# A residual quantiser whose scores, residual and codeword sum are built in PSUM

## Chip, cores, metric

One core of a Trainium2 chip. The metric is device time of one launch in microseconds (us), the median of several runs. "Faster" or "slower" needs 2%.

Codes in the profile's views: PE is TensorE (PEld its weight loads), DVE VectorE, ACT ScalarE, POOL GpSimd and SP SyncE; "L696" is line 696 of the kernel. PSUM is the memory into which the kernel's matmuls write (pool `pp`), SBUF the one that holds its other tiles. "Granted clock" is the share of full clock that TensorE was given.

## The reference, cut to what matters

The program chains four residual blocks on a tensor of 4 images x 128 channels x 64 x 64 tokens. Only the last one is touched by the change: residual vector quantisation of the normalised tokens through 8 codebooks of 1024 words of 128 channels.

```python
for i in range(8):
    cb = codebooks[i]                                  # 1024 x 128
    d = sum(res * res, -1, keepdims=True) - 2.0 * einsum('ne,ke->nk', res, cb) \
        + sum(cb * cb, -1)[None, :]
    idx = argmin(d, axis=-1)
    dec = cb[idx]
    res = res - dec
    quant = quant + dec
# output: x + quant
```

Each stage needs the residual that the stage before left, so the 8 stages of a token are a chain. Different tokens are independent.

## The kernel before

The last layer takes tokens in groups of 512, two groups at a time, and each group in four tiles of 128 tokens. There are 4 x 8 groups x 8 stages x 4 = 1024 tiles. The stage, with cuts marked:

```python
def stage(self, i):
    sq = wp.tile([P, CH], F32, name="sq", bufs=2)
    nc.scalar.activation(sq, self.res, AF.Square)
    # ... n2 = -r.r of each token by four 128x1 matmuls, copied to nr2 ...
    pd = pp.tile([P, CH], F32, name="pd", bufs=1)
    for t in range(nt):
        ts = slice(t * P, (t + 1) * P)
        pe = pp.tile([P, NCODE], F32, name="pe", bufs=3)
        for h in range(NCODE // CH):
            hs = slice(h * CH, (h + 1) * CH)
            nc.tensor.matmul(pe[:, hs], self.res[:, ts], cbT[:, i, hs], start=True, stop=True)
        # minus the distance: 2 r.c - r.r - c.c
        d = wp.tile([P, NCODE], F32, name="d")
        nc.scalar.activation(d, pe, AF.Identity, bias=nr2[:, t : t + 1], scale=2.0)
        eng = nc.gpsimd if t % 2 else nc.vector
        eng.tensor_tensor(d, d, cb2[:, i, :], ALU.subtract)
        mx = wp.tile([P, 8], F32, name="mx")
        nc.vector.max(mx, d)
        idx = wp.tile([P, 8], U32, name="idx")
        nc.vector.max_index(idx, mx, d)
        dec = wp.tile([P, P], F32, name="dec")
        nc.gpsimd.indirect_dma_start(out=dec, ...)      # gathers 128 codewords
        nc.tensor.transpose(pd[:, ts], dec, cst.ident)
    # quant = pd, later quant += pd on VectorE (0.68 us)
    if i < NCB - 1:
        nc.vector.tensor_tensor(self.res, self.res, pd, ALU.subtract)
```

The order in which an engine runs its instructions is not that of this text. A scheduler decides it when the program is built, by priority and by its own guess of what is ready when. Each engine then works through its list.

## Time and profile before

| | before |
|---|---|
| time, us (median of 4 runs) | 18549.4 |
| the quantiser's part, from its first score matmul to the end | about 4240 |
| per tile | 4.14 |
| VectorE busy there | 81% |
| TensorE busy there, mean granted clock | 73%, 0.74 |

The groups, the window sums and a stretch of timeline are shown in the prediction. The view of waits from 15000 us to the end, 3.55 of the quantiser's 4.24 ms (who waited for whom: total us, times, longest us):

```profile
ACT d L701 <- PE pe L696: 843.2, 610, 4.9
...
ACT sq L682 <- DVE res L722: 703.0, 186, 7.9
...
POOL dec L711 <- DVE idx L709: 602.6, 256, 3.4
PE pd L716 <- DMA dec<-in_codebooks,idx: 556.7, 265, 4.6
...
PE pe L696 <- DVE res L722: 368.9, 186, 3.1
```

No single wait stands out. Every engine waits for the next link of the round trip at some time, and none is full.

### The profile page before, as it was taken

What the parts mean: (1) busy time and instruction counts of PE and PEld (TensorE: products, weight loads), DVE (VectorE), ACT (ScalarE), POOL (GpSimd) and SP (SyncE); (2) the same over time, 40 slices, a digit from 0 to 9 for tenths busy, and PEclk for the clock granted to TensorE, in tenths of its full rate; (3) what the DMA queues carried; (4) which work ended last, traced back from release to release, by engine and by line L of the source; (5) the groups of instructions that cost most, each with busy time, mean ns of one, the idle gap of its engine ahead of it and who ended that gap; (6) DMA issues with size and microseconds to landing.
All of it is one profiled execution on the core that took longest, in us unless ns stands there. A gap on an engine that the chain in (4) does not pass through costs nothing. (4 is left out here: it accounts for less than half of the span.)

```text
span 18551.7 us, 160743 instructions
## 1 busy us (share of the span) xinstructions
PE 14014.2 (76%) x63834; PEld 4562.7 (25%) x63834; DVE 15474.9 (83%) x11162; ACT 12396.8 (67%) x8354; POOL 4830.7 (26%) x2586
## 2 busy tenths in 40 slices
PE   6767776677778778787787877877777777777777
PEld 2222322223111111111111111111112333333333
DVE  7978788787888888888888888888888888888888
ACT  2323232333999999999999999999998323333332
POOL 4646465461000000000000000000001555555555
PEclk8888888888999999999999999999999777777777
DMA  0000000000000000000000000000000000000000
GB/s 19 0 0 0 0 0 0 0 0 2 1 1 1 1 1 1 1 1 1 1 1 1 1 1 1 1 1 1 1 1 12 19 17 18 18 18 18 18 19 18
DMA packets 42034, 99.52 MB, mean 5 GB/s; under 512 B 18368, under 2 KB 19136, under 8 KB 40768
## 3 DMA queue, kind: packets, MB, share of 16 engines
q0 software_dynamic: 32768, 67.17, 1.4%
q1 hardware_dynamic: 6208, 19.49, 0.3%
q8 instruction: 501, 8.21, 0.2%
q10 hardware_dynamic: 2304, 2.58, 0.0%
q14 instruction: 253, 2.07, 0.0%
HBM read 80.78 MB, written 8.39 MB: 5 GB/s over the span
## 5 line engine op out<-in xcount | busy, mean ns | idle before, releaser
L622 ACT ACTIVATE a<-pad,nw 128x2048 f32<-128x2048 f32 x5120 | 9706.1, 2000 | 18.7 <-PE acc L589 15.0
L589 PE MATMUL acc<-a,sel 128*32 128x512 f32 x40960 | 7012.0, 596 | 1974.7 <-ACT a L622 1974.7
L613 DVE SCALAR_TENSOR_TENSOR m<-pad,w,m 128x2048 f32<-128x2048 f32 x3072 | 6996.1, 2347 | 0.2
L589 PEld LDWEIGHTS acc<-a,sel 128*32 128x32 f32 x40960 | 1517.1, 109 | 7266.8 <-ACT a L622 4924.3
L696 PE MATMUL pe<-cbT,res 128*128 128x512 f32 x4096 | 2634.1, 780 | 496.4 <-DVE res L722 427.8
L664 POOL MEMSET minus<- 128x1 f32 x1 | 0.1, 99 | 9752.0 <-DVE xs L630 9752.0
L701 ACT ACTIVATE d<-pe,nr 128x1024 f32<-128x1024 f32 x1024 | 1131.6, 1114 | 2102.5 <-PE pe L696 968.2
L611 DVE TENSOR_SCALAR m<-pad,w 128x2048 f32<-128x2048 f32 x1024 | 1271.2, 1283 | 1498.6 <-PE acc L589 1498.6
L310 POOL TENSOR_TENSOR y<-y,hc 128x1024 f32<-128x1024 f32 x512 | 1435.8, 2804 | 1130.7 <-DVE hc L309 1123.2
L299 PE MATMUL pc<-xs,w_c 128*128 128x512 f32 x2048 | 1186.3, 709 | 694.6 <-DVE hc L309 694.6
L307 ACT COPY state<-h 128x1 f32<-128x1 f32 x512 | 97.7, 191 | 2112.6 <-DVE h L306 2112.6
L711 POOL DMA_INDIRECT dec<-in_codebooks,idx x1024 | 1146.0, 1119 | 1115.9 <-DVE idx L709 698.7
L707 DVE MAX8 mx<-d 128x8 f32<-128x1024 f32 x1024 | 1221.2, 1216 | 205.6 <-POOL d L705 201.2
L705 POOL TENSOR_TENSOR d<-d,cb 128x1024 f32<-128x1024 f32 x512 | 1210.8, 2366 | 621.1 <-ACT d L701 604.0
L696 PEld LDWEIGHTS pe<-cbT,res 128*128 128x128 f32 x4096 | 918.4, 251 | 1471.7 <-issue 1303.9
L306 DVE TENSOR_TENSOR_SCAN h<-da,state,db 128x1024 f32<-128x1024 f32 x384 | 1242.8, 3236 | 23.2 <-ACT da L301 0.5
L299 PE MATMUL pb<-xs,w_b 128*128 128x512 f32 x2048 | 1092.4, 657 | 194.9 <-DVE db L303 194.7
L709 DVE FIND_INDEX8 idx<-mx,d 128x8 uint32<-128x1024 f32 x1024 | 1238.9, 1219 | 0.0
L589 PE MATMUL acc<-m,sel 128*32 128x512 f32 x8192 | 1138.8, 592 | 1.2 <-DVE m L613 1.2
L705 DVE TENSOR_TENSOR d<-d,cb 128x1024 f32<-128x1024 f32 x512 | 740.7, 1455 | 144.8 <-ACT d L701 144.8
L716 PE MATMUL pd<-ident,dec 128*128 128x128 f32 x1024 | 346.9, 339 | 653.6 <-DMA dec<-in_codebooks,idx 639.8
L299 PEld LDWEIGHTS pc<-xs,w_c 128*128 128x128 f32 x2048 | 405.1, 214 | 1405.6 <-DVE hc L309 1025.9
(200 smaller groups left out, 9148.2 us busy)
## 6 DMA issues: line engine op xcount, KB each, us to landing
dec<-in_codebooks,idx POOLq DMA_INDIRECT x1024, 2.6
xs<-in_x SPq DMA_DIRECT2D x4, 2048.0 KB, 15.6
out<-quant SPq DMA_DIRECT2D x32, 256.0 KB, 2.0
cbT<-in_codebooksT ACTq DMA_DIRECT2D x4, 512.0 KB, 10.1
cbT<-in_codebooksT SPq DMA_DIRECT2D x4, 512.0 KB, 10.3
w<-in_adder SPq DMA_DIRECT2D x1, 576.0 KB, 3.6
fc2T<-in_fc2T ACTq DMA_DIRECT2D x1, 64.0 KB
projT<-in_projT ACTq DMA_DIRECT2D x1, 64.0 KB, 7.7
```

Of the source, the lines that this page charges most:

```text
L299: nc.tensor.matmul(ps[:, c], w[:, n, :], xs[:, c], start=True, stop=True)
L306: nc.vector.tensor_tensor_scan(h, da, db, first, ALU.mult, ALU.add)
L310: nc.gpsimd.tensor_tensor(y, y, hc, ALU.add)
L589: nc.tensor.matmul(acc[quad * j : quad * (j + 1), bk, :], sel[:, quad - 1 - i : 2 * quad - 1 - i], parts[j][:, bk * CH : (bk + 1) * CH], s ...
L611: nc.vector.tensor_scalar(m3, win(k, r0, rh), wk, None, ALU.max)
L613: nc.vector.scalar_tensor_tensor(m3, win(k, r0, rh), wk, m3, ALU.max, ALU.add)
L622: nc.scalar.activation(a.rearrange("p (h w) -> p h w", w=SIDE), win(k, r0, rh), AF.Abs, bias=nw[:, f, k : k + 1],)
L696: nc.tensor.matmul(pe[:, hs], self.res[:, ts], cbT[:, i, hs], start=True, stop=True)
L705: eng.tensor_tensor(d, d, cb2[:, i, :], ALU.subtract)
L707: nc.vector.max(mx, d)
L709: nc.vector.max_index(idx, mx, d)
L711: nc.gpsimd.indirect_dma_start(out=dec, out_offset=None, in_=table, in_offset=bass.IndirectOffsetOnAxis(ap=idx[:, 0:1], axis=0), element_o ...
```

## The change

The intent: ScalarE's pass over the scores and the subtraction on VectorE or GpSimd vanish. TensorE puts -c.c/2 into PSUM as a first matmul and adds r.c to it; VectorE's max and index search read PSUM. The residual and the sum of codewords are accumulated in PSUM too, by multiplying each gathered tile with minus identity and with identity. Score tiles have two PSUM buffers in place of three, since the residual and the sum now take room there too. Comments that the change strips are left out, as is the setup of `half` and `row`.

```diff
         def __init__(self, b, c):
             ...
-            self.quant = wp.tile([P, CH], F32, name="quant")
+            self.left = pp.tile([P, CH], F32, name="left")
+            nc.tensor.matmul(self.left, cst.ident, self.res, start=True, stop=False, ...)
+            self.quant = pp.tile([P, CH], F32, name="quant")
+            nc.tensor.matmul(self.quant, zero, self.res, start=True, stop=False, ...)

         def stage(self, i):
-            (square, n2 matmuls, nr2)
-            pd = pp.tile([P, CH], F32, name="pd", bufs=1)
+            last = i == NCB - 1
             for t in range(nt):
-                pe = pp.tile([P, NCODE], F32, name="pe", bufs=3)
+                pe = pp.tile([P, NCODE], F32, name="pe")          # bufs=2
+                for h in range(NCODE // CH):
+                    nc.tensor.matmul(pe[:, hs], row[:, i, :], half[:, hs], start=True, stop=False)
                 for h in range(NCODE // CH):
-                    nc.tensor.matmul(pe[:, hs], self.res[:, ts], cbT[:, i, hs], start=True, stop=True)
-                d = ...; nc.scalar.activation(d, pe, ...); eng.tensor_tensor(d, d, cb2[:, i, :], ALU.subtract)
+                    nc.tensor.matmul(pe[:, hs], self.res[:, ts], cbT[:, i, hs], start=False, stop=True)
-                nc.vector.max(mx, d); nc.vector.max_index(idx, mx, d)
+                nc.vector.max(mx, pe); nc.vector.max_index(idx, mx, pe)
                 nc.gpsimd.indirect_dma_start(out=dec, ...)
-                nc.tensor.transpose(pd[:, ts], dec, cst.ident)
-            (quant += pd and res -= pd on VectorE)
+                if not last:
+                    nc.tensor.matmul(self.left[:, ts], dec, minus, start=False, ...)
+                nc.tensor.matmul(self.quant[:, ts], dec, cst.ident, start=False, ...)
+            if not last:
+                self.res = wp.tile([P, CH], F32, name="res")
+                nc.scalar.copy(self.res, self.left)
```

More of the change, by code (lines that the diff above doesn't have):

```diff
@@ L648, in layer3 @@
     mean, rstd = group_stats(tc, cst, xs, cp, "l3")
-    cb2 = cp.tile([P, NCB, NCODE], F32, name="cb2")
+    half = cp.tile([P, NCODE], F32, name="half")
+    nc.gpsimd.memset(half, 0.0)
+    pick = cp.tile([P, 2 * NCB - 1], F32, name="pick")
+    nc.gpsimd.memset(pick, 0.0)
+    nc.gpsimd.memset(pick[:, NCB - 1 : NCB], -0.5)
     with tc.tile_pool(name="l3s", bufs=2) as sp, tc.tile_pool(
-        name="l3sp", bufs=2, space=PSUM
+        name="l3sp", bufs=1, space=PSUM
     ) as pp:
+        ph = pp.tile([NCB, NCODE], F32, name="ph")
         for i in range(NCB):
@@ L657, in layer3 @@
             for h in range(NCODE // CH):
-                p2 = pp.tile([P, CH], F32, name="p2")
+                hs = slice(h * CH, (h + 1) * CH)
                 nc.tensor.matmul(
-                    p2, cst.ones, sq[:, h * CH : (h + 1) * CH], start=True, stop=True
-                )
-                nc.vector.tensor_copy(cb2[:, i, h * CH : (h + 1) * CH], p2)
-    minus = cp.tile([P, 1], F32, name="minus")
-    nc.gpsimd.memset(minus, -1.0)
+                    ph[:, hs], pick[:, NCB - 1 - i : 2 * NCB - 1 - i], sq[:, hs],
+                    start=i == 0, stop=i == NCB - 1,
+                )
+        nc.vector.tensor_copy(half[0:NCB, :], ph)
+    row = cp.tile([P, NCB, P], F32, name="row")
+    nc.vector.tensor_copy(row, cst.ident[:, 0:NCB].unsqueeze(2).to_broadcast([P, NCB, P]))
+    minus = cp.tile([P, P], F32, name="minus")
+    nc.vector.tensor_scalar(minus, cst.ident, -1.0, None, ALU.mult)
+    zero = cp.tile([P, P], F32, name="zero")
+    nc.gpsimd.memset(zero, 0.0)
     wp = ctx.enter_context(tc.tile_pool(name="l3w", bufs=4))
+    dp = ctx.enter_context(tc.tile_pool(name="l3d", bufs=8))
     pp = ctx.enter_context(tc.tile_pool(name="l3p", bufs=2, space=PSUM))
@@ L677, in __init__ @@
             normalize(nc.gpsimd, self.res, xs[:, b, self.at[1]], mean, rstd, b)
-            self.quant = wp.tile([P, CH], F32, name="quant")
-        def stage(self, i):
-            sq = wp.tile([P, CH], F32, name="sq", bufs=2)
-            nc.scalar.activation(sq, self.res, AF.Square)
-            n2 = pp.tile([P, nt], F32, name="n2", bufs=1)
-            for t in range(nt):
-                nc.tensor.matmul(
-                    n2[:, t : t + 1], sq[:, t * P : (t + 1) * P], minus, start=True, stop=True
-                )
-            nr2 = wp.tile([P, nt], F32, name="nr2")
-            nc.vector.tensor_copy(nr2, n2)
-            pd = pp.tile([P, CH], F32, name="pd", bufs=1)
+            self.left = pp.tile([P, CH], F32, name="left")
+            nc.tensor.matmul(
+                self.left, cst.ident, self.res, start=True, stop=False, skip_group_check=True
+            )
+            self.quant = pp.tile([P, CH], F32, name="quant")
+            nc.tensor.matmul(
+                self.quant, zero, self.res, start=True, stop=False, skip_group_check=True
+            )
+        def stage(self, i):
+            last = i == NCB - 1
             for t in range(nt):
                 ts = slice(t * P, (t + 1) * P)
-                pe = pp.tile([P, NCODE], F32, name="pe", bufs=3)
+                pe = pp.tile([P, NCODE], F32, name="pe")
                 for h in range(NCODE // CH):
@@ L696, in stage @@
                     nc.tensor.matmul(
-                        pe[:, hs], self.res[:, ts], cbT[:, i, hs], start=True, stop=True
+                        pe[:, hs], row[:, i, :], half[:, hs], start=True, stop=False
                     )
-                d = wp.tile([P, NCODE], F32, name="d")
-                nc.scalar.activation(
-                    d, pe, AF.Identity, bias=nr2[:, t : t + 1], scale=2.0
-                )
-                eng = nc.gpsimd if t % 2 else nc.vector
-                eng.tensor_tensor(d, d, cb2[:, i, :], ALU.subtract)
-                mx = wp.tile([P, 8], F32, name="mx")
-                nc.vector.max(mx, d)
-                idx = wp.tile([P, 8], U32, name="idx")
-                nc.vector.max_index(idx, mx, d)
-                dec = wp.tile([P, P], F32, name="dec")
+                for h in range(NCODE // CH):
+                    hs = slice(h * CH, (h + 1) * CH)
+                    nc.tensor.matmul(
+                        pe[:, hs], self.res[:, ts], cbT[:, i, hs], start=False, stop=True
+                    )
+                mx = dp.tile([P, 8], F32, name="mx")
+                nc.vector.max(mx, pe)
+                idx = dp.tile([P, 8], U32, name="idx")
+                nc.vector.max_index(idx, mx, pe)
+                dec = dp.tile([P, P], F32, name="dec")
                 nc.gpsimd.indirect_dma_start(
@@ L715, in stage @@
                 )
-                nc.tensor.transpose(pd[:, ts], dec, cst.ident)
-            if i == 0:
-                nc.vector.tensor_copy(self.quant, pd)
-            else:
-                nc.vector.tensor_tensor(self.quant, self.quant, pd, ALU.add)
-            if i < NCB - 1:
-                nc.vector.tensor_tensor(self.res, self.res, pd, ALU.subtract)
+                if not last:
+                    nc.tensor.matmul(
+                        self.left[:, ts], dec, minus, start=False, stop=i == NCB - 2,
+                        skip_group_check=True,
+                    )
+                nc.tensor.matmul(
+                    self.quant[:, ts], dec, cst.ident, start=False, stop=last,
+                    skip_group_check=True,
+                )
+            if not last:
+                self.res = wp.tile([P, CH], F32, name="res")
+                nc.scalar.copy(self.res, self.left)
         def finish(self):
             b, cs = self.at
-            nc.gpsimd.tensor_tensor(self.quant, self.quant, xs[:, b, cs], ALU.add)
-            nc.sync.dma_start(out=io["out"][:, b, cs], in_=self.quant)
+            o = wp.tile([P, CH], F32, name="o")
+            nc.vector.tensor_tensor(o, xs[:, b, cs], self.quant, ALU.add)
+            nc.sync.dma_start(out=io["out"][:, b, cs], in_=o)
     for b in range(NB):
```

## The prediction

> **What bounds the kernel now.** I read the page from the top, then the sums by window for the last layer, then a stretch of its timeline. The change touches only the last layer, the quantiser. Its first score matmul starts at 14304.6 us and the kernel ends at 18551.7, so it owns about 4.24 of 18.55 ms. It is 1024 tiles of 128 tokens (4 images, 32 groups in all, 8 codebooks, 4 tiles each): 4.14 us per tile. A change of 2% (371 us) needs 0.36 us per tile.
>
> The costliest groups on the page, those of the quantiser (columns: busy time and mean duration; then idle time ahead and its releaser):
>
> ```profile
> L696 PE MATMUL pe<-cbT,res 128*128 128x512 f32 x4096 | 2634.1, 780 | 496.4 <-DVE res L722 427.8
> L701 ACT ACTIVATE d<-pe,nr 128x1024 f32<-128x1024 f32 x1024 | 1131.6, 1114 | 2102.5 <-PE pe L696 968.2
> L711 POOL DMA_INDIRECT dec<-in_codebooks,idx x1024 | 1146.0, 1119 | 1115.9 <-DVE idx L709 698.7
> L707 DVE MAX8 mx<-d 128x8 f32<-128x1024 f32 x1024 | 1221.2, 1216 | 205.6 <-POOL d L705 201.2
> L705 POOL TENSOR_TENSOR d<-d,cb 128x1024 f32<-128x1024 f32 x512 | 1210.8, 2366 | 621.1 <-ACT d L701 604.0
> L709 DVE FIND_INDEX8 idx<-mx,d 128x8 uint32<-128x1024 f32 x1024 | 1238.9, 1219 | 0.0
> L705 DVE TENSOR_TENSOR d<-d,cb 128x1024 f32<-128x1024 f32 x512 | 740.7, 1455 | 144.8 <-ACT d L701 144.8
> ```
>
> The reader should see two things. L696 has 4096 records for 1024 tiles of two matmuls: a 128x512 fp32 matmul is two instructions. And DVE's three groups alone are 3.1 us per tile of the 4.14. The sums by window (busy us of each engine, then granted clock):
>
> ```profile
> core 0: us, PE busy (x) PEld busy (x) DVE busy (x) ACT busy (x) POOL busy (x), PEclk, DMA share, GB/s
> 16000.00:17500.00 1500.00, 1094.89 (x2528) 527.47 (x2527) 1213.09 (x1518) 455.00 (x451) 869.29 (x564) 0.74 0.07 18
> ```
>
> DVE is busy 81% and PE 73% at a mean granted clock of 0.74; neither is full. The stage is bound by a mix of DVE work and the round trip score, distance, max, index, gather, transpose, residual, with two groups of tokens in flight. The timeline shows what 0.74 is made of:
>
> ```profile
> 16998.36 0.34 PEld L696 LDWEIGHTS pe<-cbT,res 128*128 128x128 f32 x1 [0.52 <-issue]
> 16999.21 0.34 PEld L696 LDWEIGHTS pe<-cbT,res 128*128 128x128 f32 x1 [0.52 <-issue]
> ...
> 17002.59 0.19 PEld L696 LDWEIGHTS pe<-cbT,res 128*128 128x128 f32 x1 [0.27 <-issue]
> 17003.02 0.19 PEld L696 LDWEIGHTS pe<-cbT,res 128*128 128x128 f32 x1 [0.24 <-issue]
> 17003.45 0.14 PEld L716 LDWEIGHTS pd<-ident,dec 128*128 128x128 f32 x1 [0.24 <-issue]
> 17003.87 0.27 PE L716 MATMUL pd<-ident,dec 128*128 128x128 f32 x1
> 17003.98 1.88 PE L696 MATMUL pe<-cbT,res 128*128 128x512 f32 x4
> ```
>
> Weight loads, one per matmul instruction, are 0.85 us apart at 16998 and 0.43 at 17002.6: the clock flips between half and full. The steps from one matmul start to the next confirm it (429 ns or 853 ns, little between), and a transpose of 128 columns is followed 109 ns later (17003.87 to 17003.98). So full-clock costs are 0.429 us per 128x512 instruction and 0.109 per 128x128 one. The mean of 780 ns on the page mixes both clocks and the drain, and must not be used as a rate.
>
> **What the Trainium skill says.** "TensorE: Matmul & The Clock Gate", Part 1, says that the array runs at half clock unless recently busy, judged in windows of 3413 ns. The trace agrees: its clock records hold only 1.0 and 0.5, in stretches that are multiples of 3.41 us; in the quantiser the windows before a rise to full were all but fully busy, and a fall followed a window under about half busy. "FP8 and Floating Point Precision", TensorE Precision Notes, says true fp32 takes four passes; two instructions of 429 ns for 512 columns agree with two passes each. "VectorE: DVE Perf Modes", the TRN2 errata table, charges a PSUM source 120 cycles where SBUF pays 58; the trace disagrees for this size: L303, which reads 1024 elements beside PSUM, takes 1212 ns at the median, the SBUF-only L705 on DVE 1219. "DMA: Bandwidth & Descriptors", anatomy of the SWDGE path, fits 2.0 us plus bytes over 436e3; for 64 KB that is 2.15 us, while the gathers here land 2.4 at least and 2.6 at the median after their issue begins.
>
> **The change, part by part, per tile.**
> Removed: the ACT pass (1.11 us), the subtraction (1.46 on DVE or 2.37 on POOL, alternately), and a quarter of the per-stage work: square, norm matmuls, two DVE updates of 0.68. DVE keeps the max and the search: 1.21 plus 1.28 with its match load, 0.08 overlapped, 2.41 us. It falls from 3.37 busy (3451.5 over 1024) to 2.4, with slack. ACT keeps one 0.6 us copy per four tiles, POOL only the gather and the normalisations.
> Added on PE: the row matmuls that put minus c.c/2 into PSUM are full 128x128 by 512 fp32 ones, as costly as the score: two matmuls, four instructions, 1.72 us. One transpose becomes two true fp32 products (residual and codeword sum), four instructions of 0.109. PE per tile at full clock: 8 x 0.429 + 4 x 0.109 = 3.87 us, against 4 x 0.429 + 0.109 + 2 x 0.11 (its share of the norm matmuls, seen 111 to 112 ns apart) = 2.05 now. That floor alone gives 1024 x 3.87 = 3.96 ms. The gain on DVE is therefore capped at 0.28 ms (1.5%), whatever else happens.
>
> Then the order. In the built program PE runs, for tile k+2: row matmuls, then the two products with tile k's gathered codewords, then the scores of k+2. PE is in order, so the scores of k+2 cannot pass the gather of k. PSUM has room for two score tiles, not three. The loop from the start of the last score instruction of k to the same of k+2, at full clock:
> - last matmul to its end 0.59, start of DVE 0.04: 0.63
> - max and search: 2.41, at 3.04
> - search end to start of the gather's issue: 0.76, the commonest gap in the trace (searches and issues lined up one by one; a few have 0.27): 3.80
> - issue on POOL 0.94 when undisturbed: 4.74
> - issue end to weight load of the waiting product: 1.54, 6.28
> - weight load 0.11, four products 0.44: 6.83
> - three more score instructions: 1.29, giving 8.11.
> The row matmuls of k+2 lie beside the gather and cost nothing here. So 8.11 for two tiles, 4.06 us per tile, just over the PE floor of 3.87. PE would be 95% busy, hence at full clock.
>
> Per pair of groups (16 of them): four seed matmuls (residual times identity, and zeros), eight instructions, 3.4 us of PE; the two normalisations of 2.1 us stand between gathers on POOL. At the seam the codeword sum must be read by DVE before its bank is seeded again. I take 4.5 us per pair, 72 us. Setup loses 16 short DVE copies and gains small constants; about nothing.
> Sum: 1024 x 4.06 = 4157, plus 72, is 4229, against 4236 now. The change trades DVE work for PE work and lands where it was. Jitter only adds to a loop with no third tile, so I put 30 to 40 us on top: **18580 us**.
>
> **Rivals.**
> First, DVE bound: if DVE were the whole limit, 2.41 us per tile would give 2.5 ms and 16.8 ms in all. For it speaks DVE's 81%; against it that PE needs 3.87 at best. I rule it out.
> Second, PE bound: if the gather starts 0.27 after the search, the loop drops to 7.62 for two and PE's 3.87 rules; with the seams 4.03 to 4.05 ms, about 18370.
> Third, a longer round trip: if landings stay at the median 2.6 rather than 2.48 and searches in PSUM cost 60 cycles more each (the skill's table), the loop gains 0.12 + 0.13 and the period becomes 4.19: +130 us, about 18700.
> Fourth, PE falls to half clock: 7.7 us per tile and over 22 ms if it stayed so. Against it: at half clock PE is the bound, so fully busy, which in this trace brings the clock back. Spells after a seam are possible: ten microseconds at half clock lose five, 80 us over 16 seams.
>
> **Range and chances.** The floor of PE gives the low end, the long round trip with cold spells the high end: 18370 to 18880. Faster by 2% would need under 3.78 us per tile, below the floor: 0.03. Slower by 2% needs 4.5 us per tile, half a microsecond of loop latency that I have missed per tile: 0.12. Within 2%: 0.85.
>
> **What would show it.** PE about 95% busy in the quantiser with clock near 1.0; matmul steps of 429 ns; DVE near 58% with MAX8 and FIND_INDEX8 near 1.21 us; PE's main wait on the gather at the product with the residual, short (about 0.2 us a tile); about 0.76 from search to issue. A PE that never waits makes the second rival right; a clock well under 0.95 the fourth; longer DVE or gather durations the third. The prediction is wrong if a tile takes under 3.85 or over 4.45 us.

## The result, and the profile after

| | before | after |
|---|---|---|
| time, us (median of 4 runs) | 18549.4 | 18704.4 |
| ratio to before | 1 | 1.0085 (1.0071 to 1.0099) |
| quantiser, per tile, us | 4.14 | 4.29 |
| TensorE busy in the quantiser, granted clock | 73%, 0.74 | 95%, 1.00 |
| VectorE busy in the quantiser | 81% | 60% |

A ratio is the mean time of one kernel's runs over that of the other's of the same rounds, so it is not quite the ratio of the medians. By the 2% rule the two are the same; the interval says the change is slower by 0.7 to 1.0%. It also came out correct.

The costliest groups of the changed kernel, from its page, the same columns as in the prediction:

```profile
L721 DVE MAX8 mx<-pe 128x8 f32<-128x1024 f32 x1024 | 1262.4, 1233 | 1689.0 <-PE pe L717 1689.0
L717 PE MATMUL pe<-cbT,res 128*128 128x512 f32 x4096 | 1936.8, 595 | 0.0
L712 PE MATMUL pe<-half,row 128*128 128x512 f32 x4096 | 1928.6, 592 | 0.0
...
L725 POOL DMA_INDIRECT dec<-in_codebooks,idx x1024 | 970.4, 948 | 3364.0 <-DVE idx L723 2249.7
...
L723 DVE FIND_INDEX8 idx<-mx,pe 128x8 uint32<-128x1024 f32 x1024 | 1252.9, 1224 | 0.0
```

The mean of a 128x512 instruction fell from 780 to 595 ns. The instruction is the same; the array now runs at full clock. The row matmuls of L712 cost as much as the scores of L717. VectorE waits 1689 us for scores. The same window as before in the window sums:

```profile
core 0: us, PE busy (x) PEld busy (x) DVE busy (x) ACT busy (x) POOL busy (x), PEclk, DMA share, GB/s
...
16000.00:17500.00 1500.00, 1427.79 (x4157) 661.97 (x4156) 893.21 (x1060) 45.14 (x77) 352.31 (x360) 1.00 0.07 18
```

TensorE is at 95% and VectorE at 60%. One turn of the round trip, picked from the timeline of the changed kernel (start, duration, engine, line, operation; other instructions left out):

```profile
16992.68 1.88 PE L717 MATMUL pe<-cbT,res 128*128 128x512 f32 x4
...
16994.60 1.23 DVE L721 MAX8 mx<-pe 128x8 f32<-128x1024 f32 x1 [1.78 <-PE pe L717]
...
16995.87 0.09 DVE L723 MATCH_VALUE_LOAD idx<-mx,pe 128x8 f32 x1
16995.95 1.23 DVE L723 FIND_INDEX8 idx<-mx,pe 128x8 uint32<-128x1024 f32 x1
...
16997.93 0.95 POOL L725 DMA_INDIRECT dec<-in_codebooks,idx  x1 [3.40 <-DVE idx L723]
...
16998.38 1.88 PE L712 MATMUL pe<-half,row 128*128 128x512 f32 x4
...
17000.64 0.30 PEld L731 LDWEIGHTS left<-minus,dec 128*128 128x128 f32 x2 [1.21 <-DMA dec<-in_codebooks,idx]
...
17001.19 1.88 PE L717 MATMUL pe<-cbT,res 128*128 128x512 f32 x4
```

Scores of tile k begin at 16992.68, max at 16994.60, the search ends at 16997.18, the gather is issued at 16997.93, the product with it begins at 17000.64, the scores of tile k+2 at 17001.19. That is 8.51 us for two tiles in this turn. The row matmuls at 16998.38 lie inside the gather. The wait is short (1.21 us on the weight load, 0.4 on the array) and it comes at nearly every tile, as the view of waits over the whole quantiser tells (879 and 103 waits of weight loads for a gather, of 1024 tiles; the 103, before the sum's product, are left out):

```profile
POOL dec L725 <- DVE idx L723: 2249.7, 649, 8.4
DVE mx L721 <- PE pe L717: 1689.0, 1024, 8.5
...
PEld left L731 <- DMA dec<-in_codebooks,idx: 798.0, 879, 3.6
...
PE left L731 <- DMA dec<-in_codebooks,idx: 160.0, 396, 2.8
```

The scattered waits of before have become one loop: max waits for scores, the gather for the search, the product for the gather, and TensorE's list has the next scores behind that product.

### The profile page after: what moved, and what is told of

It is laid out like the page before. It is cut to its first block, busy times and chain, and to the rows that moved or that the text cites. A ratio compares the mean times of both kernels' runs of the same rounds, so it can differ in the third digit from the quotient of the medians.

```text
span 18701.1 us, 167504 instructions
## 1 busy us (share of the span) xinstructions
PE 15099.9 (81%) x68826; PEld 5007.4 (27%) x68826; DVE 14625.6 (78%) x9933; ACT 11237.2 (60%) x7298; POOL 3402.7 (18%) x2045
## 3 DMA queue, kind: packets, MB, share of 16 engines
q10 hardware_dynamic: 2304, 2.58, 0.0%
## 5 line engine op out<-in xcount | busy, mean ns | idle before, releaser
L741 ACT COPY res<-left 128x512 f32<-128x512 f32 x224 | 131.3, 586 | 4242.4 <-PE left L731 4140.1
L721 DVE MAX8 mx<-pe 128x8 f32<-128x1024 f32 x1024 | 1262.4, 1233 | 1689.0 <-PE pe L717 1689.0
L717 PE MATMUL pe<-cbT,res 128*128 128x512 f32 x4096 | 1936.8, 595 | 0.0
L712 PE MATMUL pe<-half,row 128*128 128x512 f32 x4096 | 1928.6, 592 | 0.0
L725 POOL DMA_INDIRECT dec<-in_codebooks,idx x1024 | 970.4, 948 | 3364.0 <-DVE idx L723 2249.7
L723 DVE FIND_INDEX8 idx<-mx,pe 128x8 uint32<-128x1024 f32 x1024 | 1252.9, 1224 | 0.0
L712 PEld LDWEIGHTS pe<-half,row 128*128 128x128 f32 x4096 | 778.5, 190 | 976.0 <-issue 972.4
L717 PEld LDWEIGHTS pe<-cbT,res 128*128 128x128 f32 x4096 | 704.1, 191 | 506.8 <-issue 506.8
L309 DVE TENSOR_TENSOR hc<-h,pc 128x1024 f32<-128x1024 f32 x512 | 621.8, 1214 | 106.2 <-POOL y L310 59.3
```

The costliest lines, as they stand in the source:

```text
L712: nc.tensor.matmul(pe[:, hs], row[:, i, :], half[:, hs], start=True, stop=False)
L721: nc.vector.max(mx, pe)
L723: nc.vector.max_index(idx, mx, pe)
L725: nc.gpsimd.indirect_dma_start(out=dec, out_offset=None, in_=table, in_offset=bass.IndirectOffsetOnAxis(ap=idx[:, 0:1], axis=0), element_o ...
```

## The experiments

Theory: the pace is the round trip with two tiles in flight, 8.38 us at the median from one max to that of the second tile after it (4.19 per tile, seams between pairs of groups added). TensorE's own 3.87 us per tile is a floor just beneath it. Main rival: TensorE is the limit and its waits are incidental. The experiments start from the changed kernel unless the text says otherwise. All gave correct results. They ran in two batches of four, each on one chip, beside runs of the kernel before there (18539.6 and 18542.3 us); ratios are to those.

| run | us | ratio to before | interval |
|---|---|---|---|
| the change | 18704.4 | 1.0085 | 1.0071 to 1.0099 |
| e1 products later | 18339.7 | 0.9891 | 0.9874 to 0.9907 |
| e2 bf16 row | 17416.9 | 0.9398 | 0.9382 to 0.9413 |
| e3 no sum, three score tiles | 18565.2 | 1.0018 | 1.0001 to 1.0034 |
| e4 scores only | 18398.7 | 0.9926 | 0.9909 to 0.9942 |
| e5 search twice | 18851.0 | 1.0168 | 1.0151 to 1.0185 |
| e6 no sum, products later | 18097.9 | 0.9760 | 0.9743 to 0.9776 |
| e7 all three | 17094.1 | 0.9220 | 0.9204 to 0.9235 |
| e8 bf16 row, products later | 17128.5 | 0.9240 | 0.9224 to 0.9255 |

### e1: the products emitted two tiles later

```diff
-                (left and quant products with dec, here)
+                waiting.append((self, i, t, dec))
+                while len(waiting) > 2:
+                    fold(*waiting.pop(0))      # the same two products, and the copy of res after t == 3
```

The pairs are emptied before `finish`. The built program has the same TensorE instructions, with the products with tile k now behind the scores of k+2.

> Same instructions as the changed kernel, but the two products with a gathered codeword are emitted after the scores two tiles on, so the scores of tile k+2 no longer wait for the gather of k. Theory (the round trip with two tiles in flight sets 8.38 us per two tiles): three in flight make the trip 10.1/3 = 3.4 us per tile, below the 3.87 us of TensorE work, so TensorE becomes full: 3.87 plus about 0.1 for seams, some 18370 us in all. Rival (TensorE is the limit already and its waits for the gather are incidental): no change, 18700.

Measured 18339.7. Window sums of e1:

```profile
16000.00:17000.00 1000.00, 996.39 (x3023) 497.81 (x3022) 648.85 (x771) 32.76 (x56) 257.22 (x263) 1.00 0.07 19
```

and its TensorE timeline:

```profile
16996.02 1.88 PE L718 MATMUL pe<-half,row 128*128 128x512 f32 x4
16997.74 1.88 PE L723 MATMUL pe<-cbT,res 128*128 128x512 f32 x4
16999.46 0.38 PE L744 MATMUL left<-minus,dec 128*128 128x128 f32 x2
16999.68 0.39 PE L748 MATMUL quant<-ident,dec 128*128 128x128 f32 x2
16999.90 1.88 PE L718 MATMUL pe<-half,row 128*128 128x512 f32 x4
```

TensorE is busy 99.6% and a tile takes 3.88 us (16996.02 to 16999.90), the floor of the prediction. The run is 30 us under the figure expected; the mean period with seams is 3.93 us per tile, where 3.97 was expected. Taking the wait out of TensorE's way without changing an instruction of it gained 1.9% on the changed kernel, far outside the intervals above if just short of the 2%. So in the changed kernel the wait for the gather was the pace and not incidental.

### e2: the row in three bf16 parts

```diff
-    half = cp.tile([P, NCODE], F32, name="half")           # -c.c/2 in rows 0 to 7
+    half = cp.tile([P, NCODE], BF16, name="half")          # high, middle, low parts of it
+                                                           # in rows i, 32 + i, 64 + i
-    row = cp.tile([P, NCB, P], F32, name="row")            # ones in row i
+    row = cp.tile([P, NCB, P], BF16, name="row")           # ones in rows i, 32 + i, 64 + i
```

One bf16 matmul sums the three parts, so the row costs one pass for each half of the scores where fp32 takes two instructions of two passes each.

> The row that adds -c.c/2 is built from three bf16 parts in one bf16 pass: 2 x 0.215 us per tile in place of 4 x 0.429. The build also lets the scores of k+2 go ahead of the products with k. TensorE work falls to 2.58 us per tile, VectorE's max and search are 2.6. Theory: three tiles in flight, trip 8.8/3 = 2.94, plus seams 3.05 per tile, about 17430 us at full clock. Rival (TensorE, now under 90% busy, loses its clock for long stretches): 3.5 us per tile or more, 17900 and up. If the row matmuls were hidden behind the gather and the order did not count: 18700.

Measured 17416.9. The timeline of e2 has the row as two instructions in all:

```profile
16002.38 0.59 PE L727 MATMUL pe<-half,row 128*128 128x512 bf16 x2
...
16002.81 1.88 PE L732 MATMUL pe<-cbT,res 128*128 128x512 f32 x4
```

They take 0.43 us (16002.38 to 16002.81) against 1.72. The mean period is 3.02 us per tile, expected 3.05. The window sums of e2:

```profile
16000.00:17000.00 1000.00, 915.22 (x3184) 466.17 (x3247) 837.24 (x998) 42.13 (x72) 335.37 (x342) 0.99 0.09 25
```

TensorE is at 92% with a clock of 0.99, so the rival of a lost clock falls. As the row became short, the scheduler put the scores of k+2 ahead of the products with k by itself. This run therefore mixes a shorter TensorE list with the freed order; e1 has the order alone.

### e3: no codeword sum, three score tiles, order as it was

```diff
-            self.quant = pp.tile(...); (its seed and its products)
+            self.first = self.res
...
-                pe = pp.tile([P, NCODE], F32, name="pe")
+                pe = pp.tile([P, NCODE], F32, name="pe", bufs=3)
...
-            nc.vector.tensor_tensor(o, xs[:, b, cs], self.quant, ALU.add)
+            nc.vector.tensor_tensor(o, self.first, self.left, ALU.subtract)
+            nc.vector.tensor_tensor(o, o, xs[:, b, cs], ALU.add)
```

> The codeword sum is no longer accumulated; it is taken at the end as first residual minus last. That frees two PSUM banks for a third score tile and takes 0.22 us of products per tile. The build keeps the order: products with k stand ahead of the scores of k+2. Theory (order sets the loop): 8.38 - 0.22 = 8.16 per two tiles, 4.08 plus seams 4.17, about 18570. Rival (room in PSUM is the limit): TensorE's 3.65 plus seams, about 18050.

Measured 18565.2. Lined up in the trace, two tiles take 8.16 us at the median, to the figure expected. A third score tile in PSUM bought nothing, and TensorE's shorter list shows only in the 0.22 us that lay on the loop.

### e4: only the first half of the change

```diff
-            self.left, self.quant in PSUM with their seeds and products
+            self.quant = wp.tile([P, CH], F32, name="quant")
+            pd = pp.tile([P, CH], F32, name="pd")          # in stage, as in the kernel before
+                nc.tensor.transpose(pd[:, ts], dec, cst.ident)
+            (quant += pd and res -= pd on VectorE, as in the kernel before)
-                pe = pp.tile([P, NCODE], F32, name="pe")
+                pe = pp.tile([P, NCODE], F32, name="pe", bufs=3)
```

> Only the first half of the change: scores with -c.c/2 built in PSUM and searched there, but residual and sum updated on VectorE from a transposed codeword as before, three score tiles in PSUM. The build has the transpose of k ahead of the scores of k+2. Theory: loop of 6.54 + 0.11 + 0.11 + 1.29 = 8.05 per two tiles, 4.03 us, VectorE's updates adding up to 0.2: 18450 to 18650. Rival (accumulating in PSUM is what holds the changed kernel back): well under 18300.

Measured 18398.7, some 50 us below the range expected. Two tiles take 7.98 us at the median (expected 8.05), and VectorE's updates, for which I had allowed 0.2 us, added nothing to the loop: VectorE is busy 71% and does them while it would wait for scores. The first half of the change alone is thus 0.7% faster than the kernel before, and the second half turned that into 0.85% slower: on the loop, four true products stand in place of one transpose. The timeline of e4:

```profile
16996.33 0.14 PEld L723 LDWEIGHTS pd<-ident,dec 128*128 128x128 f32 x1 [1.22 <-DMA dec<-in_codebooks,idx]
...
16996.50 1.88 PE L710 MATMUL pe<-cbT,res 128*128 128x512 f32 x4
```

From the waiting weight load to the scores it has 0.17 us (16996.33 to 16996.50) and the changed kernel 0.55 (17000.64 to 17001.19); these are also the medians over all tiles. That is 0.38 of the 0.40 us between the two loops. e4 differs from the changed kernel in its third score tile too, but by e3 that bought nothing in this order.

### e5: the search done twice

```diff
+                spare = dp.tile([P, 8], U32, name="spare")
+                nc.vector.max_index(spare, mx, pe)
                 nc.vector.max_index(idx, mx, pe)
```

> The changed kernel with every index search done twice (the first into a spare tile), so 1.2 us more in the round trip of each tile and not one TensorE instruction more; VectorE work stays under 3.9 us per tile. The build answers by putting the products between the two halves of the scores of k+2. Theory (round trip): 0.63 + 2.57 + 1.2 + 0.76 + 0.95 + 1.63 + 0.55 + 0.43 = 8.72 per two tiles, 4.36 against 4.19, about 170 us longer: 18850 to 18900. Rival (TensorE sets the pace, waits incidental): unchanged within 0.3%, 18700.

Measured 18851.0, in the range. By the ratios that is 1.0168 over 1.0085, 0.8% or about 150 us, for work on an engine that was 60% busy. Lined up in the trace, two tiles take 8.72 us at the median, the figure expected. Window sums of e5:

```profile
16000.00:17000.00 1000.00, 937.47 (x2679) 420.02 (x2677) 843.15 (x1132) 29.26 (x50) 224.52 (x231) 1.00 0.06 17
```

VectorE has room left at 84%, TensorE stays at 94%, and still it costs time: what lies in the loop counts, whichever engine it is on. It costs less than 0.6 us per tile (half of the 1.2 added to a loop of two tiles) because the scheduler moved the products between the halves of the scores.

### e6 to e8: the limits one after the other

e6 is e3 with the products emitted three tiles later; e7 is e6 with the bf16 row of e2; e8 is e2 with the products later and the sum kept.

```diff
-                (product with dec, here)
+                waiting.append((self, i, t, dec))
+                while len(waiting) > 3:
+                    fold(*waiting.pop(0))
```

> No codeword sum, three score tiles, and now the product with k behind the scores of k+3 (the run without a sum, in another order). Theory: the order was the limit there, so now TensorE is full at 8 x 0.429 + 2 x 0.109 = 3.65 us per tile, plus seams 3.71: about 18100. Rival (order is not the limit): as the run without a sum, 18565.

Measured 18097.9. From e3 it differs in order alone, and gains 2.6%. TensorE is 99.6% busy, two tiles take 7.31 us at the median: 3.66 per tile against 3.65 expected. The third score tile that was worth nothing in e3 can be used once the order lets it.

> No codeword sum, three score tiles, products later, row in bf16: TensorE work 2.37 us per tile, below VectorE's max and search of 2.57 to 2.61. Theory: VectorE is full, 2.62 us per tile with small seams, about 17000. Rivals: TensorE at 90% loses its clock (17400 or more); gathers on GpSimd, 0.95 plus waits, stall each other (17200 or more).

Measured 17094.1, about 90 us over. It is the fastest kernel, 7.8% under the one before. VectorE's group of maxima and the window sums of e7:

```profile
L739 DVE MAX8 mx<-pe 128x8 f32<-128x1024 f32 x1024 | 1250.9, 1223 | 306.1 <-PE pe L735 188.1 <-issue 104.8
```

```profile
16000.00:17000.00 1000.00, 926.92 (x2970) 452.09 (x2969) 891.04 (x1129) 46.84 (x80) 372.96 (x379) 1.00 0.10 28
```

VectorE is at 89% and TensorE at 93% with a full clock. The period is 2.71 us where I expected 2.62. VectorE idles 306 us before a max, mostly for scores, so it is near its limit and not at it; what holds the scores back at those times I did not find out.

> The bf16 row with the codeword sum kept (two score tiles only) and products later. TensorE 2.58, VectorE 2.6, score tiles 5.0 per two: three limits within 0.1 us, so some waits of each on the other: 2.75 us per tile, about 17120. If a third score tile is what matters: as the first bf16 run, 17420.

Measured 17128.5, as expected. Against e7 it keeps the sum and two score tiles and loses 0.2%, with intervals that overlap. So with order and row mended the third score tile hardly matters. Against e2 it differs in order alone and gains 1.7% (0.9240 over 0.9398): the order that the scheduler had found in e2 by itself could still be bettered.

## Why the prediction was right

The forecast was 18580 with a range of 18370 to 18880 and "within 2%"; 18704 is in the range. By its steps:

- **TensorE's floor caps the gain.** Right: the steps between 128x512 instructions are 429 ns, and e1, where TensorE is full, shows 3.88 us per tile against 3.87 worked out.
- **VectorE falls to 2.4 busy with slack.** Right in kind: 60% busy, 58% forecast.
- **TensorE 95% busy at full clock.** Right: 1427.79 of 1500 us at 1.00. TensorE's waits on the gather, forecast at about 0.2 us a tile, come to 160.0 + 45.7 us on the array, 0.20 a tile. Here the change gained something that its description does not name: the mean clock rose from 0.74. The quantiser's clock records hold 245 falls to half clock before (95% of them after a window of 3.41 us in which TensorE was busy for under 55%) and six after.
- **The loop over two tiles.** The mechanism is right (e1, e3, e5); its length was put at 8.11 (the terms add up to 8.12) and measured 8.38 at the median. Two terms were too short. Max and search were put at 2.41 and take 2.569 in every tile. The gap from the end of the gather's issue to the waiting weight load was put at 1.54 and is 1.63 at the median. Together 0.25 of the 0.27, the rest being rounding and scatter. The other terms hold: 0.04 from scores to max, 0.76 to the issue, 0.946 for the issue, 0.55 for load and products.
- **Seams and jitter.** 72 us and some 35 predicted. The mean over two tiles is 8.579 against the median 8.384; half of that difference over 1022 pairs is 100 us. About 60 of it lie in the six steps from max to max around each of the 15 changes of pair, the other 40 are spread over the rest of the tiles. So the seams were put a little too long and the jitter about right.

The sum: the loop adds 0.27 / 2 x 1024 = 138 us, and 100 for seams and jitter in place of 107 takes 7 off. These terms account for about 131 us, against the 124 by which 18580 was short. So the centre was missed by two durations put too short, and not by a wrong step in the argument; no large errors cancelled.

The search term was mis-sized by how it was measured. I took both durations from the kernel before, where VectorE rarely searched for a maximum it had just found (one of its 1024 match loads follows directly on the max that it needs). This is VectorE's timeline there:

```profile
16994.05 0.09 DVE L709 MATCH_VALUE_LOAD idx<-mx,d 128x8 f32 x1
16994.12 1.22 DVE L709 FIND_INDEX8 idx<-mx,d 128x8 uint32<-128x1024 f32 x1
16995.26 0.07 DVE L709 MATCH_VALUE_LOAD idx<-mx,d 128x8 f32 x1
16995.31 1.22 DVE L709 FIND_INDEX8 idx<-mx,d 128x8 uint32<-128x1024 f32 x1
```

Two searches stand in a row, for maxima found earlier, and the second match load starts at 16995.26, 0.08 us before the search ahead of it ends at 16995.34. That overlap I carried over. In the changed kernel the match load waits for the max just ahead of it: 16994.60 + 1.23 is 15.83, and it starts at 15.87. Over all tiles the gap is 0.035 after the end in place of 0.083 before it, 0.118 us; the longer max (1.233), match load (0.092) and search (1.224) make up the other 0.04.

That this comes of the wait and not of PSUM, e5 shows, where each maximum is searched for twice from the same PSUM tile:

```profile
16000.60 1.23 DVE L721 MAX8 mx<-pe 128x8 f32<-128x1024 f32 x1 [1.60 <-PE pe L717]
16001.87 0.09 DVE L724 MATCH_VALUE_LOAD spare<-mx,pe 128x8 f32 x1
16001.95 1.22 DVE L724 FIND_INDEX8 spare<-mx,pe 128x8 uint32<-128x1024 f32 x1
16003.09 0.07 DVE L725 MATCH_VALUE_LOAD idx<-mx,pe 128x8 f32 x1
```

The first match load, which needs the max ahead of it, starts 0.035 us after the max ends, the second 0.083 us before the first search ends; so it is in all 1024 tiles, to 3 ns. The one match load of the kernel before that followed on its own max, with its tiles in SBUF, started 0.034 us after it. Nor is it the kind of instruction ahead: in e7, 493 match loads follow the max of another tile, and they start 0.082 us before its end at the median.

Of the rivals, the third (a longer round trip, about 18700) is what happened, though half of its reason was wrong. The landings do stay long (2.58 us at the median from the start of the issue to the weight load, where the loop had 2.48). But PSUM as a source did not cost a search 60 cycles more: a max took 17 ns more on the mean, and about 5 ns like for like, since in the kernel before a max that started on an idle VectorE took 1.228 us, and here all do, at 1.233. The first, VectorE bound, falls (60% busy). The second, TensorE bound, is refuted for the changed kernel by e1 and e5. Its figure comes true in e1, but not for the reason it named (a gather 0.27 us after the search: 83 of 1024 tiles have that). The fourth, a lost clock, falls: between 14.3 and 18.45 ms the clock records hold five spells at half clock, of 3.4 us each.

Where did the expected gain go? VectorE was relieved of 0.8 us per tile (3.37 busy before; now 0.595 of 4.29, or 2.55) and ScalarE of 1.1. A part went to TensorE, whose list grew from 2.05 to 3.87 us per tile at full clock, and the rest was lost to an order in which only two tiles can be in flight.

## What to carry to other kernels

Before moving work to an engine that looks idle, add up its work per tile at full clock, and then close the loop: in the built order of the in-order engine, find what stands between an input and the instruction that waits for it, and count the tiles in flight. If a wait for a transfer stands ahead of independent work in that list, emit it later; here that cost nothing and gained 1.9%, and another buffer without it gained nothing. A constant added in PSUM costs as much as the matmul that it is added to unless it is made in fewer passes: three bf16 parts in one contraction did it for a quarter.

## What the Trainium skill lacked or had wrong

- "VectorE: DVE Perf Modes", "The DRAIN you can't avoid", reports for a chain of eight tensor_copy operations that a semaphore after each costs nothing extra. That does not carry over to a max and its search: in e5 a match load that needs the max just ahead of it starts 0.035 us after that ends, one that follows a search and needs nothing of it starts 0.083 us before its end. No page gives this step of 0.118 us, nor the 2.569 us of a max followed by its own search, which I had put at 2.41.
- "VectorE: DVE Perf Modes", the TRN2 errata table, charges a PSUM source 62 cycles more than SBUF. MAX8 over 1024 fp32 elements took 1233 ns from PSUM and, where it too started on an idle engine, 1228 from SBUF (1216 on the mean of all); FIND_INDEX8 took 1224 and 1219.
- "DMA: Bandwidth & Descriptors", anatomy of the SWDGE path: its fit gives 2.15 us for a 64 KB transfer; the gathers landed 2.4 us after the start of their issue at least and 2.5 at the median. The fit is not for gathers in particular, and no page has a figure for one. The page also lacks what comes before: from the end of the index search to the start of the issue 0.76 us in most tiles, 0.27 in some. What goes with the two values can be read from the semaphores in the packed trace: in the changed kernel all 83 gathers with 0.27 wait in their own instruction for VectorE's semaphore, and all 917 with 0.76 for TensorE's, the wait for the search being, for nearly all of these, a separate instruction ahead of them. The other runs divide the same way; none set out to change it, so that this is the cause is not shown.
- No page gives the time of an fp32 matmul, which has to be worked out from the four passes that the prediction cites: the runs show two instructions of 429 ns for 512 columns and, where the product is a true one, two of 109 ns for 128 (a transpose has one). Nor does a page show that a constant row can be added in one bf16 pass of three parts: 0.43 us per tile in e2 against 1.72 in fp32, with a correct result.
